# Feed-forward of a decoder layer: gatherings and sortings as two half DMAs on SyncE and GpSimd, with halves exchanged, and the next inputs' reads issued after the sums

## The chip, the cores and the metric

The kernel runs on one core of a Trainium2 chip. A core has a matrix engine (TensorE, PE in the profile, with its weight loads as PEld), a vector engine (VectorE, DVE), a scalar engine (ScalarE, ACT), a general engine (GpSimd, POOL) and an engine that only issues and waits (SyncE, SP). Each works through its own instructions in order; semaphores tie them together. Transfers (DMAs) are issued here by SyncE and GpSimd, and run on the 16 DMA engines of the core. SBUF, the core's memory, has 128 partitions; PE writes to PSUM, whence VectorE or ScalarE copies.

The metric is the device time of one execution in microseconds: the median of the runs is 610.52 us (three runs, 610.5 to 610.85).

## The reference, cut to what matters

The layer is self-attention, a decaying recurrence over a context, and a feed-forward, each with a residual and a layer norm. The change lies in the feed-forward, over 2048 tokens of 512 features:

```python
gate_w = spline_reconstruct(gate_cp, INTER, HIDDEN)   # cubic interpolation of few control points
up_w = spline_reconstruct(up_cp, INTER, HIDDEN)       # INTER = 2048, HIDDEN = 512
down_w = spline_reconstruct(down_cp, HIDDEN, INTER)
gate = jnp.einsum('bsh,ih->bsi', hidden_states, gate_w)
up = jnp.einsum('bsh,ih->bsi', hidden_states, up_w)
inter = jax.nn.silu(gate) * up
return jnp.einsum('bsi,hi->bsh', inter, down_w)
```

The weights are piecewise cubic polynomials along their rows. The kernel uses this: a row times a vector is a few exact products near the breaks of the polynomial plus moments of the vector over the pieces.

## The kernel before, in words

**Plan.** `ffn_plan` (line 55) is Python that runs before the kernel is built. It orders the 2048 intermediate features into 16 tiles of 128 and makes the tables: `up_taps` and `down_taps` (for the weights), `mom_f` (for the moments of the inputs) and `sum_f` (for the moments of the intermediates).

**Blocks.** The tokens are worked in four blocks b = 0..3 of 512 tokens (`GT`). All arrays are float32. The attention comes first; its last stage also makes the inputs of blocks 0 and 1.

**Inputs of a block.** `inputs(b)` (line 700) transposes the normed tokens on PE, writes them to memory off the core (`xd`; mostly issued by GpSimd, a few rows by SyncE), forms moments on PE and writes these too (`md`, by GpSimd). The input tile `xg` of a block, 128 partitions by 8 x 512 numbers, is read back from both: `windows` (line 683) issues four reads of `xd`, into 44 partitions of each half, and `moments` (line 694) two reads of `md`, into 20 partitions of each half. All six are on SyncE. For blocks 0 and 1 they are issued at once; for blocks 2 and 3 they are put into the list `reads`. `xg` has two buffers.

**Loop over the blocks** (lines 940 to 972; the order of the instructions of each engine is the order in which this Python calls them, since `Ordered` keeps the program order):

- For j = 0..7, `gate_up` (line 842) makes two tiles of `inter`: four matmuls for the gate and four for the up projection from `xg[:, j]`, silu on ScalarE, product on VectorE. `gather` (line 858) then issues, on SyncE, one DMA for each of the two tiles: it spreads the tile's 128 partitions over 16 partitions (r, r+8, ...) of `nat`, eight rows of 512 numbers to each. In blocks 1 and 2, one piece of `inputs(b+1)` follows each j; block b therefore makes the inputs of block b+1.
- Then the list `reads` is emptied: in blocks 1 and 2 this issues the six reads of the next block's `xg`.
- For t = 0..15, `exact` (line 865) adds four matmuls of tile t to the four outputs `y`. In blocks 1 to 3, at t = 0..3 the chain `outcome` (line 907) of the block before is started: transposes on PE, residual and norm on VectorE, ScalarE and GpSimd (`va`, `rs`), and a DMA `out<-o` on SyncE.
- At t = 7 come `residual(b)` (line 921), which later lets GpSimd copy the residual in 36 instructions (`x2p<-x`), and four calls of `into_sums` (line 875): eight matmuls `ps_s` each from `nat` and the table `sf`, a copy out of PSUM to `sum`, and a DMA `fin<-sum` on SyncE which sorts the 128 rows into 32 partitions of `fin` (called `sorted_` in the code).
- After t = 15, `finish` (line 894) adds eight matmuls `y<-fin` from the sorted sums and copies `y` out of PSUM.

The lines that the change edits are these:

```python
nc.sync.dma_start(out=nats[b, g][r::NSUM], in_=inters[b, t])   # gather
nc.sync.dma_start(out=sorted_[b][v::ND], in_=o)                # into_sums
while reads:                                                   # the loop, before t = 0
    reads.pop(0)()
```

Here `NSUM` is 8, `ND` is 4 and `K2` is 64. A DMA on SyncE takes one of eight completion semaphores in turn, so an issue waits until the DMA eight places before it has landed.

Of the kernel before, what the change touches and what calls it, by code (L numbers as in the profile page):

```python
# [17 lines left out]
P = 128  # L18
# [10 lines left out]
ND = 4  # L29
NTILE = INTER // P  # L30
NSUM = 8
# [5 lines left out]
K2 = 64  # L37
# [17 lines left out]
def ffn_plan():  # L55
# [9 lines left out]
    t = np.linspace(0.0, NCTRL - 1.0, n, dtype=np.float64)  # L65
# [10 lines left out]
    for d in range(ND):  # L76
# [4 lines left out]
        for j in range(-1, 18):  # L81
            b = np.clip(np.ceil(at + period * j - 1e-9).astype(int), 0, INTER)
# [56 lines left out]
    def covers(u, d):  # L139
        return range(BASE[u][d], BASE[u][d] + NSEG - (u == 0))  # L140
# [47 lines left out]
    def taps(sample, k):  # L188


        f = sample * step - k
        b = np.stack(
            [
                -0.5 * f + f**2 - 0.5 * f**3,
                1.0 - 2.5 * f**2 + 1.5 * f**3,
                0.5 * f + 2.0 * f**2 - 1.5 * f**3,
                -0.5 * f**2 + 0.5 * f**3,
            ]
        )
        return b, np.stack([np.clip(k + a, 0, NCTRL - 1) for a in (-1, 0, 1, 2)])  # L200
# [12 lines left out]
    for t in range(NTILE):  # L213
# [3 lines left out]
        for s in range(5):  # L217
            a, b = edges[2 * s], edges[2 * s + 1]
# [13 lines left out]
        b, i = taps(rows * D + places[:, None], piece[rows * D + within])  # L232
        b = b * (places < D)[None, :, None]
# [12 lines left out]
    for t in range(NTILE):  # L246
        rows = parts[t]
        for d in range(ND):
            q = slice(d * 32, (d + 1) * 32)
            sample = outs[d][None, :] * INTER + rows[q, None]  # L250
            dn_b[:, q, t * P : (t + 1) * P], dn_i[:, q, t * P : (t + 1) * P] = taps(sample, piece[sample])
        for p, i in enumerate(rows):
            u = p % NSUM
            r = t % NSUM + NSUM * (p // NSUM)
            for d in range(ND):
                if d == p // 32:
                    continue
                s = seg_of[d][i]
                if i in ALONE:
                    free = [s for s in range(NSEG) if s not in covers(0, d) or segs[d][s][0] == segs[d][s][1]]  # L260
                    taken = alone.setdefault(d, [])
                    taken.append(i)
                    x = free[(len(taken) - 1) // 4] * 4 + (len(taken) - 1) % 4
                    sums[r, t // NSUM * NSUM + u, x * ND + d] = 1.0
                else:
                    x = (s - BASE[u][d]) * 4 + np.arange(4)
                    sums[r, t // NSUM * NSUM + u, x * ND + d] = fact[d][s][1][i - segs[d][s][0]]
    for u in range(NSUM):
        for d in range(ND):
            col = slice((NTILE + d) * P, (NTILE + d + 1) * P)  # L270
            for s in range(NSEG):
                a, b = segs[d][BASE[u][d] + s]
                at, inner = fact[d][BASE[u][d] + s][0], np.full(4, min(a, INTER - 1))
                if u == 0 and (s not in covers(0, d) or a == b):
                    at, inner = np.zeros(4), np.zeros(4, np.int64)
                    for k in range(min(4, len(alone[d]))):
                        at[k] = inner[k] = alone[d].pop(0)
                r = ((u % 2 * 16 + s * 4 + np.arange(4)) * 4 + u // 2)[:, None]
                c = np.arange(col.start, col.stop)[None, :]
                inner = piece[outs[d][None, :] * INTER + inner[:, None]]  # L280
                dn_b[:, r, c], dn_i[:, r, c] = taps(outs[d][None, :] * INTER + at[:, None], inner)
# [34 lines left out]
def decoder_kernel(ctx: ExitStack, tc: tile.TileContext, x, xT, ctxT, wq, wkT, wvT, woT, wdownT, wup, decay, up_taps, down_taps, mom_f, sum_f, out, plan):  # L316
    nc = tc.nc
# [27 lines left out]
    nc = Ordered(tc)  # L345
    units, chains = [], []

    def slot():

        for c in list(chains):  # L350
            if next(c, c) is c:
                chains.remove(c)

    def fill(n):

        for i in range(n):
            if units:
                next(units[0][1])
                units[0][2] -= 1
                if not units[0][2]:  # L360
                    units.pop(0)
            if i % 2:
                slot()
                some_taps()
# [205 lines left out]
    def output(n, qc):  # L570

        ps = ps_mm.tile([P, D], F32, tag="mm", name="ps_o")
        for c in range(DC):
            nc.tensor.matmul(
                ps,
                lhsT=yTs[n][c // 2][:, c % 2, qc * P : (qc + 1) * P],
                rhs=w_o[:, c, :],
                start=(c == 0),
                stop=(c == DC - 1),
            )  # L580
            if c < DC - 1:
                yield
        h1 = rows.tile([P, D], F32, tag="row", name="h1")
        s1 = small.tile([P, 1], F32, tag="s1", name="s1")
        nc.vector.scalar_tensor_tensor(h1, ps, 1.0, xs[n][qc], ALU.mult, ALU.add, accum_out=s1)
        chains.append(norms(n, qc, h1, s1))
        yield
# [93 lines left out]
    xgs, reads = {}, []  # L681
# [70 lines left out]
    for s, (g, bb, quad) in enumerate(steps):  # L752
# [8 lines left out]
        if quad == 0 and n:  # L761
            load_rows(n - 1)
            o = [["o", output(n - 1, qc), DC] for qc in range(2)]
# [76 lines left out]
    inters, ys, sorted_, xps, nats = {}, {}, {}, {}, {}  # L840

    def gate_up(b, j):

        pgs, pus = [], []
        for w, pool, tag, to in ((wg, ps_mm, "mm", pgs), (wu, ps_big, "big", pus)):
            for h in range(2):
                at = slice(h * K2, (h + 1) * K2)
                ps = pool.tile([P, GT], F32, tag=tag, name="pg" if w is wg else "pu")
                nc.tensor.matmul(ps, lhsT=w[at, j * P : (j + 1) * P], rhs=xgs[b][at, j, :], start=True, stop=True)
                to.append(ps)  # L850
        for h in range(2):
            sg = work.tile([P, GT], F32, tag="sg", name="sg")
            nc.scalar.activation(sg, pgs[h], AF.Silu)
            inter = work.tile([P, GT], F32, tag="inter", name="inter", bufs=NTILE)
            nc.vector.tensor_tensor(inter, pus[h], sg, ALU.mult)
            inters[b, 2 * j + h] = inter

    def gather(b, t):

        g, r = t // NSUM, t % NSUM  # L860
        if not r:
            nats[b, g] = work.tile([P, NSUM, GT], F32, tag=f"nat{g}", name="nat", bufs=1)
        nc.sync.dma_start(out=nats[b, g][r::NSUM], in_=inters[b, t])

    def exact(b, t):

# [8 lines left out]
    def into_sums(b, v):  # L875

        if v == 0:
            sorted_[b] = late.tile([P, ND, GT], F32, tag="fin", name="fin")
        acc = ps_mm.tile([P, GT], F32, tag="mm", name="ps_s")
        for g in range(NTILE // NSUM):  # L880
            for a in range(2):
                u = 2 * v + a
                nc.tensor.matmul(
                    acc[a * K2 : (a + 1) * K2, :],
                    lhsT=sf[:, g * NSUM + u, :],
                    rhs=nats[b, g][:, u, :],
                    start=(g == 0),
                    stop=(g == NTILE // NSUM - 1),
                )
        o = work.tile([P, GT], F32, tag="inter", name="sum", bufs=NTILE)  # L890
        (nc.vector.tensor_copy if v % 2 else nc.scalar.copy)(o, acc)
        nc.sync.dma_start(out=sorted_[b][v::ND], in_=o)

    def finish(b):
        y = late.tile([P, ND, GT], F32, tag="ys", name="ys")
# [40 lines left out]
    def settle():  # L936
        while chains:
            slot()

    for b in range(NG):  # L940
        if 0 < b < NG - 1:
            units.append(["i", inputs(b + 1), 2 * DC])
        for j in range(NTILE // 2):
            gate_up(b, j)
            gather(b, 2 * j)
            gather(b, 2 * j + 1)
            if b:
                slot()
                fill(1)
        if b == 0:  # L950
            fill(2 * DC)
        while reads:
            reads.pop(0)()
        for t in range(NTILE):
            exact(b, t)
            if b and t < TC:
                chains.append(outcome(b - 1, t))
            slot()
            if b == 0 and t < 5:
                slot()  # L960
            if b == 0 and t == 4:
                settle()
                done.close()
                late = ffn["mom"] = ctx.enter_context(tc.tile_pool(name="late", bufs=1, side="right"))
            if t == 7:
                settle()
                chains.append(residual(b))
                for v in range(NSUM // 2):
                    into_sums(b, v)
        assert not units  # L970
        finish(b)
    for t in range(TC):
# [55 lines left out]
```

## Time and profile before

The profiled execution took 612.27 us, with a span of 610.5 us from the first to the last instruction and a mean granted TensorE clock of 0.993.

| engine | busy us | share of the span | instructions |
|---|---|---|---|
| PE | 584.3 | 96% | 3346 |
| PEld | 288.8 | 47% | 3346 |
| DVE | 334.5 | 55% | 742 |
| ACT | 276.9 | 45% | 820 |
| POOL | 210.1 | 34% | 479 |

The feed-forward begins at 401.3 us. Its stages, by PE, start at these times (us):

| block | `gate_up` | `exact` t=0 | sums `ps_s` | `exact` t=8 | `finish` |
|---|---|---|---|---|---|
| 0 | 401.27 | 423.15 | 431.83 | 438.85 | 445.93 |
| 1 | 449.56 | 471.28 | 482.03 | 489.05 | 497.75 |
| 2 | 501.35 | 523.07 | 533.83 | 540.85 | 550.06 |
| 3 | 555.36 | 569.30 | 581.05 | 588.07 | 595.15 |

DMAs of the feed-forward, from the table of issues:

| DMA | issued by | count | KB each |
|---|---|---|---|
| `nat<-inter` (gatherings) | SyncE | 64 | 256 |
| `fin<-sum` (sortings) | SyncE | 16 | 256 |
| `xg<-xd` (windows, four blocks) | SyncE | 8 and 8 | 616 and 88 |
| `xg<-md` (moments, four blocks) | SyncE | 8 | 320 |
| `out<-o` | SyncE | 16 | 256 |
| `xd<-x2T` | GpSimd | 16 | 250 to 256 |
| `md<-mom` | GpSimd | 4 and 4 | 512 and 128 |

How to read the rows of the profile: a group of instructions is told as engine, line, operation, output tile, inputs, shape, number, and in brackets the idle time of the engine before it with what ended that. All instructions stand under line 308, a helper that records them, so tiles tell them apart. A table of stretches gives the busy time of each engine, the granted TensorE clock, the mean busy share of the 16 DMA engines and the GB/s that they moved. The chain of waits goes back from the last instruction to what released it, step by step.

### The profile page before, as it was taken

How to read it: one execution, taken by the hardware profiler on the slowest of the kernel's cores; microseconds unless marked ns; L12 is line 12 of the kernel's file. 1: busy time of each engine (PE TensorE's matmuls, PEld its weight loads, DVE VectorE, ACT ScalarE, POOL GpSimd, SP SyncE). 2: the span in 40 equal slices, each digit the busy share in tenths (PEclk: the TensorE clock that was granted, in tenths of full speed). 3: DMA queues.
4: the chain of work that ended last, by engine and by line, in shares of the span. 5: the costliest groups of instructions: out<-in, count | busy, mean ns of one | idle time of the engine just before them, and what ended most of it. 6: DMA issues, size and time to landing. Idle time of an engine off the chain costs nothing.

```text
span 610.5 us, 9688 instructions
## 1 busy us (share of the span) xinstructions
PE 584.3 (96%) x3346; PEld 288.8 (47%) x3346; DVE 334.5 (55%) x742; ACT 276.9 (45%) x820; POOL 210.1 (34%) x479
## 2 busy tenths in 40 slices
PE   8999999998999999999999898899999989999993
PEld 3544555555455555555556455444343333334432
DVE  0204545657875666786665778867635316504614
ACT  0115634647555456565556666664233214304402
POOL 0001986264636334644420301202511611350152
PEclk9999999999999999999999999999999999998998
DMA  8104253044124114314101653588129849973931
GB/s 301 52 0 155 89 182 92 20 139 138 53 68 141 35 53 160 118 52 139 47 23 53 176 141 108 156 195 177 71 71 246 226 121 236 222 208 79 217 119 69
DMA packets 39984, 75.50 MB, mean 124 GB/s; under 512 B 3936, under 2 KB 8288, under 8 KB 39936
## 3 DMA queue, kind: packets, MB, share of 16 engines
q1 hardware_dynamic: 36880, 66.94, 40.1%
q0 software_dynamic: 2048, 6.77, 3.4%
q10 hardware_dynamic: 1008, 1.18, 0.6%
q8 instruction: 26, 0.43, 0.3%
q14 instruction: 22, 0.18, 0.1%
HBM read 42.86 MB, written 11.04 MB: 88 GB/s over the span
## 4 chain that ended last, share of the span: by engine, by line
PE 72%; DVE 10%; issue 7%; DMA 5%; ACT 3%; POOL 2%; SPq 0%; POOLq 0%; DVEq 0%; ACTq 0%
PE ps_k L308 9%; PE ps_v L308 9%; PE ps_o L308 8%; PE y L308 8%; PE ps_q L308 7%; PE tr_e L308 6%; PE sc L308 5%; PE av L308 5%; PE pg L308 4%; PE pu L308 3%; DVE nmax L308 3%; PE ps_s L308 2%; DMA xg<-md 2%; ACT e L308 2%; PE ps_mom L308 2%
## 5 line engine op out<-in xcount | busy, mean ns | idle before, releaser
L308 ACT ACTIVATE e<-sc,nmax 128x256 f32<-128x256 f32 x256 | 120.3, 481 | 101.4 <-DVE nmax L308 101.3
L308 DVE TENSOR_REDUCE nmax<-sc 128x2 f32<-128x512 f32 x128 | 84.4, 681 | 73.6 <-PE sc L308 67.6
L308 POOL TENSOR_TENSOR taps<-taps 128x256 f32<-128x256 f32 (+1 forms) x144 | 89.0, 618 | 32.1 <-DMA taps<-in_down_taps 24.2
L308 PE MATMUL tr_e<-ident,e 128*128 128x128 f32 x512 | 68.3, 276 | 0.6 <-DVE eT L308 0.4
L308 PEld LDWEIGHTS tr_e<-ident,e 128*128 128x128 f32 x512 | 56.9, 140 | 25.2 <-issue 22.5
L308 PE MATMUL y<-inter,wd 32*128 32x512 f32 x512 | 63.6, 605 | 0.0
L308 PE MATMUL ps_o<-w_o,yT 128*128 128x512 f32 x128 | 60.0, 600 | 1.9 <-DVE eT L308 1.6
L308 PE MATMUL ps_k<-xT_g,w_k 128*128 128x512 f32 x128 | 58.7, 600 | 0.6 <-DVE eT L308 0.6
L308 PE MATMUL ps_v<-w_v,xT_g 128*128 128x512 f32 x128 | 58.6, 598 | 0.4 <-DVE eT L308 0.4
L308 PE MATMUL ps_q<-xT_g,w_q 128*128 128x512 f32 x128 | 58.2, 596 | 0.0
L308 POOL TENSOR_SCALAR va<-ss 128x1 f32<-128x1 f32 x32 | 7.0, 220 | 144.5 <-ACT x L308 85.8
L308 DVE TENSOR_TENSOR inter<-pu,sg 128x512 f32<-128x512 f32 x64 | 41.2, 686 | 26.6 <-PE pu L308 13.7
L308 ACT ACTIVATION_READ_ACCUMULATOR e<-sc,nmax 128x1 f32 x256 | 53.3, 208 | 0.0
L308 POOL TENSOR_TENSOR rs<-va,neghalf 128x1 f32<-128x1 f32 x48 | 28.0, 584 | 70.3 <-DVE va L308 67.6
L308 ACT ACTIVATE sg<-pg 128x512 f32<-128x512 f32 x64 | 36.1, 596 | 30.1 <-PE pg L308 29.9
L308 DVE COPY eT<-tr_e 128x512 f32<-128x512 f32 x64 | 43.7, 682 | 0.5 <-PE tr_e L308 0.4
L308 PE MATMUL av<-eT,v_g 128*32 128x256 f32 x512 | 36.7, 385 | 5.0 <-ACT eT L308 2.7
L308 PEld LDWEIGHTS y<-inter,wd 32*128 32x128 f32 x512 | 25.2, 184 | 28.9 <-issue 24.4
L308 ACT COPY eT<-tr_e 128x512 f32<-128x512 f32 x64 | 37.5, 586 | 2.4 <-PE tr_e L308 2.4
L308 PE MATMUL sc<-k_g,q_g 32*128 32x256 f32 x512 | 37.4, 401 | 0.2 <-ACT e L308 0.2
L308 POOL TENSOR_TENSOR r<-r 128x1024 f32<-128x1024 f32 x8 | 15.2, 1896 | 63.3 <-DMA r<-in_ctxT 63.3
L308 PEld LDWEIGHTS ps_v<-w_v,xT_g 128*128 128x128 f32 x128 | 23.1, 190 | 25.5 <-issue 24.3
(97 smaller groups left out, 734.0 us busy)
## 6 DMA issues: line engine op xcount, KB each, us to landing
nat<-inter SPq DMA_DIRECT2D x64, 256.0 KB
taps<-in_down_taps SPq DMA_DIRECT2D x40, 256.0 KB
taps<-in_up_taps SPq DMA_DIRECT2D x16, 384.0 KB
xg<-xd SPq DMA_DIRECT2D x8, 616.0 KB
r<-in_ctxT SPq DMA_DIRECT2D x8, 512.0 KB
x_t<-in_x SPq DMA_DIRECT2D x16, 256.0 KB
fin<-sum SPq DMA_DIRECT2D x16, 256.0 KB
out<-o SPq DMA_DIRECT2D x16, 256.0 KB
```

Source lines behind the costliest of these rows:

```text
L308: return lambda *a, **k: self.tc.keep_in_program_order(f(*a, **k))
```

## The change

Three things are edited.

- In `gather`, the one DMA becomes two. SyncE takes the tile's partitions 0 to 63 and spreads them over partitions 64+r, 72+r, ... of `nat`; GpSimd takes partitions 64 to 127 and spreads them over r, 8+r, ... below 64. So the halves change places. The table `sum_f`, whose rows stand for the partitions of `nat`, is turned by 64 rows to match.
- In `into_sums`, the sorting DMA becomes two in the same manner, and the `down_taps` rows that meet the sorted sums change halves too.
- The loop over `reads` moves from before t = 0 to the end of t = 7, behind the four calls of `into_sums`.

```diff
@@ ffn_plan
-            r = t % NSUM + NSUM * (p // NSUM)
+            r = (t % NSUM + NSUM * (p // NSUM) + P // 2) % P
...
-                r = ((u % 2 * 16 + s * 4 + np.arange(4)) * 4 + u // 2)[:, None]
+                r = (((u + 1) % 2 * 16 + s * 4 + np.arange(4)) * 4 + u // 2)[:, None]
@@ gather
-        nc.sync.dma_start(out=nats[b, g][r::NSUM], in_=inters[b, t])
+        nc.sync.dma_start(out=nats[b, g][K2 + r :: NSUM], in_=inters[b, t][:K2])
+        nc.gpsimd.dma_start(out=nats[b, g][r:K2:NSUM], in_=inters[b, t][K2:])
@@ into_sums
-        nc.sync.dma_start(out=sorted_[b][v::ND], in_=o)
+        nc.sync.dma_start(out=sorted_[b][K2 + v :: ND], in_=o[:K2])
+        nc.gpsimd.dma_start(out=sorted_[b][v:K2:ND], in_=o[K2:])
@@ the loop over the blocks
-        while reads:
-            reads.pop(0)()
         for t in range(NTILE):
             exact(b, t)
...
                 for v in range(NSUM // 2):
                     into_sums(b, v)
+                while reads:
+                    reads.pop(0)()
```

## The prediction

> **What bounds the kernel now.** I read the busy table first: TensorE (PE) is busy for 96% of the span, the next engine for 55%. So the time is PE's program order plus the few gaps in it, and a change pays only where PE stands still. Next, PE's timeline in the feed-forward, where the change lies. Columns: start, duration, instruction group, in brackets the idle time before it and what ended it.
>
> ```profile
> 482.03 7.09 PE L308 MATMUL ps_s<-nat,sf 128*64 128x512 f32 x32
> 489.05 7.15 PE L308 MATMUL y<-inter,wd 32*128 32x512 f32 x64
> 497.75 3.67 PE L308 MATMUL y<-fin,wd 128*128 128x512 f32 x8 [1.55 <-DMA fin<-sum]
> ...
> 533.83 7.09 PE L308 MATMUL ps_s<-nat,sf 128*64 128x512 f32 x32
> 540.85 7.15 PE L308 MATMUL y<-inter,wd 32*128 32x512 f32 x64
> 550.06 5.37 PE L308 MATMUL y<-fin,wd 128*128 128x512 f32 x8 [2.07 <-DMA fin<-sum]
> 555.36 1.13 PE L308 MATMUL pg<-xg,wg 64*128 64x512 f32 x4
> ```
>
> These are blocks b=1 and b=2: sums (`ps_s`), exact matmuls of t=8..15, `finish` (`y<-fin`), and the next block's `gate_up` (`pg`), which reads `xg`. Only here does PE wait for something the change touches: 1.55 and 2.07 us for the sorted sums. After the longer gap the eight `finish` matmuls took 5.37 instead of 3.67 us. Blocks 0 and 3 have no such gap: from the start of `ps_s` to the end of `finish` they need 449.56-431.83 = 17.7 and 598.69-581.05 = 17.6 us. What delays the sums is in the chain of waits (start, duration, what) and in SyncE's queue:
>
> ```profile
> 531.48 13.62 DMA xg<-md
> 545.10 0.02 issue
> 545.12 0.02 SPq L308
> 545.13 0.03 issue
> 545.16 4.76 DMA fin<-sum
> 549.93 0.14 issue
> 550.06 5.37 PE y L308 x8
> ```
>
> ```profile
> SPq L308 <- DMA xg<-md: 4.5, 2, 2.5
> SPq L308 <- DMA xg<-xd: 3.1, 2, 2.3
> ```
>
> The second fence is the queue's waits between 524 and 548 us (total, times, longest). The sums' DMAs are issued behind the six reads of the next inputs, and SyncE waits for those reads to land before it issues the later sums. So the next block's data arrive first, with time to spare, and this block's sums last.
>
> **The change, part by part.**
>
> *Reads behind the sums: what goes.* The sums no longer queue behind reads. Block 0 shows the undisturbed queue: four sum issues from 435.45 to 440.21, the last ending 8.4 us after `ps_s` began (431.83), and `finish` followed without a wait. Then blocks 1 and 2 reach their next `gate_up` 17.7 us after the start of `ps_s`: at 499.7 instead of 501.35, and at 551.5 instead of 555.36. Gain, if nothing is late next: 1.6+3.8 = 5.4 us, which is the two gaps and 1.70 us of slow matmuls.
>
> *Reads behind the sums: what is late next.* `gate_up` of block b+1 with j=0 needs both halves of `xg`, rows from the windows and from the moments, so the last of the six reads. SyncE works in order; each sum issue waits for its copy out of PSUM, which waits for PE. So the first read goes out 8.4 us after `ps_s` begins: at 490.4 (block 1) and 542.2 (block 2), where now it goes at 473.02 and 525.22. PE will want the data at 499.7 and 551.5: the cover is 9.3 us. How long do the reads take? By the table of DMA issues they move 2x88+2x616+2x320 = 2,048 KB. Nearest rows, stretches with almost only such reads in flight (the windows at 387.5, the moments at 395 with two row loads and at 541):
>
> ```profile
> 387.50:390.00 2.50, 2.50 (x10) 1.25 (x10) 2.40 (x10) 1.68 (x7) 0.56 (x1) 1.00 0.76 151
> 395.00:401.00 6.00, 5.71 (x37) 2.98 (x35) 3.15 (x10) 2.49 (x6) 1.39 (x3) 1.00 0.69 151
> 541.00:543.00 2.00, 2.00 (x20) 0.98 (x24) 0.66 (x1) 0.00 (x0) 0.83 (x4) 1.00 0.85 150
> 561.00:577.00 16.00, 16.00 (x86) 6.74 (x83) 10.42 (x22) 7.84 (x16) 1.48 (x4) 1.00 1.07 211
> ```
>
> The last number is GB/s. At 151 GB/s, 2.097 MB take 13.9 us, plus 1.2 us from issue to first data (block 3's first gathering is issued at 558.15, the DMA engines move nothing until 559.3): 15.1 us. The other end is the present itself: 525.22 to 531.48+13.62 = 545.10, 19.9 us, with the tail of the gatherings and the writes of `md` in its way, which will be done by then. I take 17. The last read then lands at 507.4 and 559.2, and PE stands 7.7 us each time. Against the present starts of `gate_up`: 507.4-501.35 = +6.0, 559.2-555.36 = +3.9. Together +9.9 us, the 5.4 us of gain already inside.
>
> *The clock after the new gaps.* The 1.55 us gap left the granted clock at 1.00; after the 2.07 us gap it was 0.69 over 549.9 to 555.36, and 1.70 us were lost. The Trainium skill ("TensorE: Matmul & The Clock Gate", section "Why this matters for your kernels") asks for no idle gaps over about 3 us. By that rule the 2.07 us gap would not explain the slow matmuls, their 1.70 us would stay, and my sum would be 1.7 higher; the row says that the gap made them slow, so I let them go with it. The new gaps of 7.7 us are past both limits: I charge each the measured 1.70 us, +3.4. Ends: nothing, and twice that each.
>
> *Gatherings in halves.* All 64 `nat<-inter` DMAs become 64 half-size ones on SyncE and 64 on GpSimd. SyncE keeps its number of issues, about 0.55 us each. GpSimd gains 64 issues; its nearest row, `md<-mom` and `xd<-x2T`, has 0.64 and 0.56 us. In a block's `gate_up` that is 16 x 0.56 = 9 us beside at least 13.9 us in which GpSimd does at most 2.3 us of work. Queued behind a half that waits for its `inter` are the `xd` writes and, in the exact loop, the norm's `va`/`rs`, which come later anyway; the late reads give `xd` time. Without this cover the norm chain is delayed, whose `h3`/`o` nobody on PE waits for until the end of the kernel. What limits a gathering is the fourth row: 211 GB/s, 16 engines more than full, so 262,144 bytes in 1.24 us a tile, while `gate_up` makes a tile in 0.87 us. A rule of the skill speaks against halves: "DMA: Bandwidth & Descriptors" ("Why a DMA increments its semaphore by 16 and not by 1") says that a DMA runs on the largest number of engines up to 16 that divides the slowest dimension of both sides. Whole gatherings write 16 partitions, halves 8: eight engines instead of sixteen. At the row's 13.2 GB/s per engine, SyncE's 131,072 bytes take 1.24 us on eight. If GpSimd's half runs on the other eight, or shared engines go faster because two queues feed them, a tile still takes 1.24 us; if both sit on the same eight at that pace, 2.5 us. I take 1.24: the row's share over full says that engines wait on each other's writes, not that each is at its own limit. In block 3 the cover is thin (16 x 1.24 after 559.3 is 579.1, sums begin at 581.05), in the others 5 us or more. Cost 0; ends -0 (no `ps_s` waits for `nat` now) and +2.
>
> *Sortings in halves.* SyncE's and GpSimd's last halves go out 8.4 us after `ps_s` begins; GpSimd's DMAs land 4.3 us after issue (`xd<-x2T`), `finish` begins 14.1 us after: 1.4 us to spare. Behind them on GpSimd are the 36 copies of `residual`, 8.4 us, today at 580.90 in block 3; they would end at 589.5+8.4 = 598 where `h` needs them at 600.07. Cost 0; if that 2 us of cover goes, as much at the end.
>
> *Tables `sum_f` and `down_taps`.* Rows change places, same sizes: 0, one answer.
>
> Sum: +9.9+3.4 = +13.3 us. The profiled execution took 612.27 us with a span of 610.5; it becomes 625.6. The median shown is 610.52, so my forecast is **623.8 us**.
>
> **Rivals.**
>
> 1. *The reads land in time (faster).* For it: the sums really are delayed by reads, and PE's gaps are named after them. If the reads ran at the 292 GB/s that the mix of 491 to 494 us reached, they would need 7.2+1.2 us, under the cover of 9.3; all 5.4 us would be gained: 605 us. It decides at a read time of about 11 us: at 10.9 the new gaps are 1.6 us and the balance is (490.4+10.9-501.35)+(542.2+10.9-555.36) = -2.3; from some 11.4 on the gaps pass 2.07 us, the clock goes too, and it is slower. Against: 15.1 us is the low end, and at 151 GB/s the windows' 1,408 KB alone take 9.5+1.2 us.
>
> 2. *Halved gatherings become the bound.* At 2.5 us a tile they end 40 us after their first data: about 14 us after the present start of `ps_s` in block 0, 12 in each of 1 and 2, 18 in block 3; some 55 us, with the late reads 55+13 more, 679 us. For it: the engine count of the skill. Against: the over-full engines above, and a second queue.
>
> 3. *No change that can be told.* The order is changed but the reads overlap the last sums enough that new gaps come to what the old ones were (a read time near 11): 610.5 us.
>
> **Numbers.** Forecast 0.86, rival 1 0.06, rival 2 0.05, rival 3 0.03. Range: read time 15.1 to 19.9 us (-3.8, +5.8), clock (-3.4, +3.4), gatherings (+2), not all at one end: 616 to 633, with about 0.15 outside. About 0.2% is what this kernel's measurement can tell from no change. Faster 0.07, same 0.03, slower 0.90.
>
> **What would show it.** Right: no wait of `y<-fin` for `fin<-sum` in blocks 1 and 2, a wait of about 8 us of `pg` (or its weight load) for `xg<-md` at the start of blocks 2 and 3, none at block 1; a granted clock under 1.00 just after; `xg<-xd` issued after `fin<-sum`. Halves right: `ps_s` without waits. Wrong: `pg` starts without a wait (rival 1), or `ps_s` waits for `nat` (rival 2), or the waits at `pg` are under 5 us.

## The result and the profile after

The changed kernel takes 644.81 us (median of four runs, 643.4 to 645.05) against 610.6 us for the kernel before: a ratio of 1.0555, 95% interval 1.0537 to 1.0573. It is slower by 34 us. The forecast had the sign, but its 623.8 us and its range up to 633 us were too low. The profiled execution took 645.03 us with a span of 643.1 us, 32.6 us more than the span before.

First the timeline of PE after the change, the lines that answer to those shown of before (start, duration, group, idle time before it and what ended that):

```profile
432.94 1.08 PE L308 MATMUL ps_s<-nat,sf 128*64 128x512 f32 x4
434.54 6.23 PE L308 MATMUL ps_s<-nat,sf 128*64 128x512 f32 x28 [0.52 <-DMA nat<-inter]
...
485.96 6.23 PE L308 MATMUL ps_s<-nat,sf 128*64 128x512 f32 x28 [1.00 <-DMA out<-o]
492.12 7.15 PE L308 MATMUL y<-inter,wd 32*128 32x512 f32 x64
499.20 3.70 PE L308 MATMUL y<-fin,wd 128*128 128x512 f32 x8
509.07 3.24 PE L308 MATMUL pg<-xg,wg 64*128 64x512 f32 x3 [6.17 <-issue]
...
547.56 7.20 PE L308 MATMUL ps_s<-nat,sf 128*64 128x512 f32 x32
...
561.77 3.70 PE L308 MATMUL y<-fin,wd 128*128 128x512 f32 x8
571.51 2.04 PE L308 MATMUL pg<-xg,wg 64*128 64x512 f32 x2 [6.04 <-DMA xg<-md]
573.75 1.19 PE L308 MATMUL pg<-xg,wg 64*128 64x512 f32 x1 [0.20 <-DMA xg<-md]
...
606.52 8.71 PE L308 MATMUL ps_s<-nat,sf 128*64 128x512 f32 x28 [4.81 <-DMA nat<-inter]
```

The waits of `finish` for the sums are gone: both `y<-fin` groups now follow without a gap and take 3.70 us. In their place `gate_up` (`pg`) of blocks 2 and 3 waits some 6 us for the inputs, and then 1.5 to 1.7 us more in its first matmuls, whose second half of `xg` lands with the last read. New are the waits of `ps_s`, worst in block 3; the forecast had `ps_s` without waits, and named such waits as a sign that it was wrong. In block 1 the row names `out<-o` as what ended the wait. `ps_s` reads only `nat` and `sf`, and the DMAs of SyncE share their completion semaphores in turn, so what it waited for is a gathering there too. In block 3 the chain of waits runs through the gatherings:

```profile
584.88 9.98 DMA nat<-inter
...
594.93 11.35 DMA nat<-inter
606.28 0.24 issue
606.52 8.71 PE ps_s L308 x28
```

The last gathering is issued on SyncE only at 594.93, when an earlier one has landed, and lands at 606.28; GpSimd's last half had landed at 601.09. In the table of stretches, here cut where the clock changes, the granted clock is the third figure from the right:

```profile
505.74:519.40 13.66, 10.33 (x20) 3.59 (x20) 1.38 (x2) 2.87 (x5) 1.77 (x3) 0.50 0.39 80
519.40:521.00 1.60, 1.60 (x10) 0.92 (x10) 1.34 (x3) 0.00 (x0) 0.34 (x1) 1.00 0.25 86
570.59:577.42 6.83, 5.72 (x12) 2.26 (x14) 0.69 (x1) 1.19 (x2) 0.50 (x1) 0.50 0.18 37
577.42:579.00 1.58, 1.58 (x10) 0.76 (x8) 1.18 (x2) 1.18 (x2) 0.51 (x2) 1.00 0.38 56
```

The clock falls to half during each gap and stays there after PE has started again at 509.07 and 571.51: for 10.3 us in block 2 and 5.9 us in block 3. PE does not work through all of that time, since it waits once more for the second half of `xg`; from there, 511.12 and 573.75, it is 8.3 and 3.7 us. And one cost lies behind all work. The kernel ends with a `DRAIN` on each engine's sequencer; the rows of GpSimd's before the change (line 1023) and after it (line 1025), and of SyncE's after it, give min/median/max in ns, then the first and last start in us:

```profile
L1023 POOLq DRAIN  x3: 40/93/2644, 606.0 to 610.2; - x3
```

```profile
L1025 POOLq DRAIN  x3: 40/93/9182, 633.1 to 642.8; - x3
L1025 SPq DRAIN  x3: 7/7/7, 636.8 to 642.6; - x3
```

GpSimd's longest starts when the last norm is issued. It took 2.644 us before, and ended about 1 us before the last output had landed. It takes 9.182 us now and ends at 642.3, while SyncE, which waits for the outputs, gets to its first `DRAIN` at 636.8. So the whole kernel waits for GpSimd's.

The 32.6 us, by comparing when PE reaches the same place in both traces (rounded rows):

| where | us |
|---|---|
| start of the kernel (the attention begins later and keeps that distance) | +1.1 |
| `ps_s` waits for `nat`: blocks 0, 1, 2, 3 | +0.7, +1.2, +0.1, +7.5 |
| waits of `finish` gone, with the slow matmuls behind the second | -1.6, -3.8 |
| `gate_up` of blocks 2 and 3 waits until both halves of `xg` are there | +7.8, +7.8 |
| half clock in these `gate_up` | +4.5, +2.3 |
| `exact` of block 3 | -0.6 |
| end of the kernel, behind PE | +5.5 |

Of the 7.5 us in block 3, 4.8 us are the wait and 2.5 us the half clock behind it (28 matmuls in 8.71 instead of 6.23 us).

### The profile page after: what moved, and what is told of

Same layout as the page of the kernel before. It is cut to its first block, busy times and chain, and to the rows that moved or that the text cites. A ratio compares the mean times of both kernels' runs of the same rounds, so it can differ in the third digit from the quotient of the medians.

```text
span 643.1 us, 9961 instructions
## 1 busy us (share of the span) xinstructions
PE 596.1 (93%) x3346; PEld 293.5 (46%) x3346; DVE 335.6 (52%) x742; ACT 277.2 (43%) x820; POOL 254.2 (40%) x559
## 5 line engine op out<-in xcount | busy, mean ns | idle before, releaser
L308 POOL DMA_DIRECT2D nat<-inter x64 | 36.3, 568 | 70.5 <-DVE inter L308 58.0
L308 PE MATMUL pg<-xg,wg 64*128 64x512 f32 x128 | 47.2, 672 | 12.4 <-DMA xg<-md 6.2
L308 PE MATMUL pu<-xg,wu 64*128 64x512 f32 x128 | 43.9, 635 | 0.0
```

What stands on the lines that cost most here:

```text
L308: return lambda *a, **k: self.tc.keep_in_program_order(f(*a, **k))
```

## The experiments

**Late reads alone.** From the kernel before:

```diff
-        while reads:
-            reads.pop(0)()
         for t in range(NTILE):
...
                     into_sums(b, v)
+                while reads:
+                    reads.pop(0)()
```

> Only the reads move behind the sums; gatherings and sortings are whole, on SyncE. Theory (three separate costs: late reads with a long slow clock, slow half gatherings, a longer end on GpSimd): the span goes from 610.5 to about 627 us: waits of finish for the sums gone (-5.3), two waits of gate_up for the reads (+12), some 10 us of half clock after them; ps_s waits for nothing, the end after the last output as before (3.3 us). Rival (the late reads cause nearly all, by pushing the gatherings too): 635 us or more, with ps_s waiting for nat. Rival (the clock costs 1.7 us for each gap, as I had it): about 621 us.

Measured: 628.36 us, ratio 1.0284 (1.0255 to 1.0312), span 627.8 us. PE's timeline in it:

```profile
496.13 3.70 PE L308 MATMUL y<-fin,wd 128*128 128x512 f32 x8
505.82 2.04 PE L308 MATMUL pg<-xg,wg 64*128 64x512 f32 x2 [6.00 <-issue]
508.15 1.19 PE L308 MATMUL pg<-xg,wg 64*128 64x512 f32 x1 [0.28 <-DMA xg<-md]
...
598.35 7.09 PE L308 MATMUL ps_s<-nat,sf 128*64 128x512 f32 x32
```

`finish` does not wait, `gate_up` waits, `ps_s` takes its 7.09 us without a wait, and the `DRAIN` is 2.644 us as before. So the late reads are worth 17 us, half of the loss, and they do not cause the slow gatherings. While PE worked, the clock was at half from 505.8 to 517.6 and again from 568.6 to 575.7.

**Halves alone.** The gather and sort edits of the change with their tables; the reads stay before t = 0.

> Only the halves; the reads stay before t = 0. Theory: ps_s waits for nat (5 us and a slow clock in block 3, about 1 us in blocks 0 and 1), the end is 5.5 us longer, no wait of gate_up for xg: 625 to 629 us. Rival (the halves only suffer where the late reads shift them): 616 us, the longer end alone.

Measured: 637.77 us, ratio 1.0453 (1.0421 to 1.0485), span 635.1 us, more than the theory said.

```profile
504.30 5.33 PE L308 MATMUL y<-fin,wd 128*128 128x512 f32 x8 [5.53 <-DMA fin<-sum]
...
542.04 1.08 PE L308 MATMUL ps_s<-nat,sf 128*64 128x512 f32 x4
544.32 6.23 PE L308 MATMUL ps_s<-nat,sf 128*64 128x512 f32 x28 [1.19 <-DMA nat<-inter]
562.82 5.08 PE L308 MATMUL y<-fin,wd 128*128 128x512 f32 x8 [5.20 <-DMA fin<-sum]
...
599.38 7.93 PE L308 MATMUL ps_s<-nat,sf 128*64 128x512 f32 x28 [4.78 <-DMA out<-o]
```

No `pg` waits. But with reads in the old place the slow gatherings delay the reads behind them, and these the sums: in block 1 the last read goes out at 486.97 instead of 483.01 and the last sum at 499.28 instead of 492.40. `finish` waits over 5 us twice. The two parts therefore do not add: 24.6 us of halves and 17.3 us of reads make 32.6 us together, since the late reads spare the halves these waits. The wait in block 3 and the `DRAIN` of 9.182 us are those of the full change.

**Late reads, with PE kept busy.** The first experiment, and after `finish`:

```diff
+        if 0 < b < NG - 1:
+            ps = ps_mm.tile([P, GT], F32, tag="mm", name="ps_fill")
+            for _ in range(16):      # 8 in the second of the two
+                nc.tensor.matmul(ps, lhsT=ident, rhs=sorted_[b][:, 0, :], start=True, stop=True)
```

> The first experiment with 16 idle matmuls of 512 columns behind finish in blocks 1 and 2, whose result nobody reads. Theory (the gap makes the clock slow, and the slow clock lasts since PE is not busy enough to leave it): the granted clock is 1.00 through gate_up, the reads land at the same place, about 10 us less than the first experiment: 617 us. Rival (gate_up is slow for another cause, such as the DMAs): no gain, 627 us.

> Late reads alone with 8 idle matmuls behind finish in blocks 1 and 2 (16 took 13.9 us each time instead of the 6.9 us I had meant, and PE was late by itself). Theory (half clock after a gap costs about 4 to 5 us in each block when nothing fills it): gate_up starts when the reads land, about 8 us after finish, at full clock; 619 to 621 us against 627.8 for the late reads alone. Rival (the clock is not the cause): 627 us or more.

Measured: 634.97 us with 16 and 625.05 us with 8 idle matmuls (one run each; spans 633.2 and 622.2 us, 627.8 us without). My first size was wrong: one float32 matmul of this form is two instructions and takes 0.86 us, so sixteen fill 13.9 us where the gap is 7.8 us. PE then was late by the filler itself, and the total says nothing on the clock. The stretches of both `gate_up` do; with 16, then with 8:

```profile
514.10:535.90 21.80, 21.80 (x100) 8.07 (x99) 11.73 (x19) 9.85 (x18) 2.26 (x4) 1.00 0.83 209
578.05:592.00 13.95, 13.95 (x67) 6.14 (x66) 9.03 (x14) 8.94 (x16) 0.00 (x0) 1.00 0.75 154
```

```profile
507.70:529.50 21.80, 21.44 (x93) 8.09 (x92) 10.90 (x17) 9.28 (x17) 2.26 (x4) 1.00 0.76 197
566.20:581.00 14.80, 14.50 (x64) 7.21 (x64) 9.76 (x15) 9.16 (x16) 0.00 (x0) 1.00 0.74 153
```

The clock is 1.00 and `gate_up` takes the 21.8 and 14 us it took before the change, with the same DMAs beside it; the last row also has the wait for the second half of `xg` in it. That the gap makes `gate_up` slow is shown. With 8 fillers the span is 5.6 us shorter than with the bare gap, though PE does 14 us of idle work. That is less than the 7 to 9 us expected, but the feed-forward of this run also began 1.1 us later. From the arrival of the second half of `xg` to the start of `exact`, blocks 2 and 3 are 4.5 and 2.4 us shorter, the size that the half clock has in the full change.

**Sortings in halves alone.** Only the sort edit with its table.

> Only the sortings in exchanged halves; gatherings whole on SyncE, reads before t = 0. Theory (the end on GpSimd grows with the number of its DMAs, 24 before and 104 after, 6.5 us for 80 of them): with 40 it is 1.3 us longer; the waits of finish for fin stay, since SyncE's halves are still behind the reads: 611.8 us. Rival (any use of GpSimd's queue late in the kernel makes the long end): 616 us.

Measured: 614.55 us, one run; span 612.8 us, 2.3 us more. The drain is 1.3 us longer, as expected; with 40 GpSimd DMAs it reads

```profile
L1024 POOLq DRAIN  x3: 40/102/3953, 608.0 to 612.5; - x3
```

Behind PE the kernel ends only 0.3 us later, since before the change the drain ended some 1 us before the last output had landed. The waits of `finish` grew by 0.6 and 0.9 us, and the feed-forward began 0.4 us later. Against the forecast's 0 for this part that is small, and from one run.

**Gatherings cut otherwise.** Four variants, with the reads before t = 0. Halves that stay in their places, gatherings and sortings (tables as before):

```diff
+        nc.sync.dma_start(out=nats[b, g][r:K2:NSUM], in_=inters[b, t][:K2])
+        nc.gpsimd.dma_start(out=nats[b, g][K2 + r :: NSUM], in_=inters[b, t][K2:])
```

> Halves on SyncE and GpSimd, but each half stays in its own half of the partitions (tables as before); reads before t = 0. To be compared with the halves that change places (635.1 us span). Theory (each half writes eight partitions and so runs on fewer DMA engines; the places do not matter): the same waits of ps_s for nat, 632 to 638 us. Rival (the exchange makes halves cross each other's ports): ps_s hardly waits, 616 to 622 us. Rival (the exchange helps): slower than 640 us.

Halves by columns, sortings whole:

```diff
+        nc.sync.dma_start(out=nats[b, g][r::NSUM, :, : GT // 2], in_=inters[b, t][:, : GT // 2])
+        nc.gpsimd.dma_start(out=nats[b, g][r::NSUM, :, GT // 2 :], in_=inters[b, t][:, GT // 2 :])
```

> Gatherings split by columns: SyncE takes the first 256 columns of all 128 partitions, GpSimd the others; sortings whole, reads before t = 0. Theory (too few engines per half): with 16 partitions written by each DMA the pace is that of whole gatherings, ps_s waits for nothing, and only the end is longer by 64 x 0.082 = 5.2 us: 616 us. Rival (two queues on the same engines slow each other): ps_s waits for nat as in the halves by partitions, 628 us or more.

The change's two gathering halves both on SyncE (`nc.sync` in both lines), and whole gatherings all on GpSimd (`nc.gpsimd` in the old line), sortings whole in both:

> Gatherings in exchanged halves, both issued by SyncE; sortings whole, reads before t = 0. Theory (a half of eight partitions runs on eight engines, and SyncE's always on the same eight): the sixteen tiles of block 3 take about 40 us instead of 20, ps_s waits 10 us or more in every block: over 650 us. The end as before (3.3 us). Rival (the slow part is GpSimd's queue or its sharing): ps_s hardly waits, about 612 to 616 us.

> Whole gatherings, all issued by GpSimd; the rest as before the change. Theory (engine count and number of GpSimd DMAs are what costs): the pace of whole gatherings stays, 1.2 us a tile, ps_s waits under 1 us, and the end is 5.2 us longer; the sums no longer stand behind gatherings in SyncE's queue: 614 to 616 us. Rival (GpSimd's queue is slow by itself): ps_s waits 5 us or more in block 3, 625 us or more.

| variant | time (one run) | span | wait of `ps_s` in block 3 | GpSimd DMAs | longest `DRAIN` |
|---|---|---|---|---|---|
| before | 610.6 (median) | 610.5 | 0 | 24 | 2.644 |
| exchanged halves | 637.77 (median) | 635.1 | 4.78 | 104 | 9.182 |
| halves in their places | 639.75 | 637.8 | 5.59 | 104 | 9.182 |
| halves by columns | 613.63 | 611.9 | 0 | 88 | 7.877 |
| exchanged halves, both on SyncE | 648.27 | 646.5 | 9.39 | 24 | 2.642 |
| whole, on GpSimd | 620.11 | 618.3 | 0 | 88 | 7.875 |

From PE's timelines, block 3, of the halves by columns and of the halves on SyncE alone:

```profile
578.23 7.09 PE L308 MATMUL ps_s<-nat,sf 128*64 128x512 f32 x32
```

```profile
616.25 7.88 PE L308 MATMUL ps_s<-nat,sf 128*64 128x512 f32 x28 [9.39 <-DMA out<-o]
```

This decides three things. Two queues are not the trouble: columns on two queues have no wait of `ps_s`. GpSimd's queue is not the trouble: whole gatherings on it have none either, and halves without GpSimd are the worst of all. The exchange is not the trouble, and no cure that can be told: the one run of straight halves lies within the runs of exchanged ones (637.11 to 640.52). What the three slow variants share is a DMA that reads 64 and writes 8 partitions.

The stretches say what that shape does. Halves on SyncE alone, in block 3, while they queue up (the last figures are the busy share of the DMA engines and GB/s):

```profile
586.00:600.00 14.00, 14.00 (x71) 5.75 (x68) 9.04 (x18) 6.71 (x13) 0.69 (x2) 1.00 0.54 127
```

The whole gatherings of the kernel before, in the same block (561 to 577), had 1.07 and 211 GB/s. So with halves only about half of the 16 DMA engines are busy, though more are queued. The trace agrees in two more ways. Of SyncE's packets mostly 8 or 9 are in flight at a time, where whole gatherings have 16 or more. And the landing of a whole gathering steps its semaphore 16 times, that of a SyncE half 8 times. For this variant the expectation was over 650 us, from 40 us for the gatherings of a block. It came out a little lower: they took 33.1 us, or 2.1 us a tile. Eight engines are faster each than sixteen (127/8 = 15.9 against 13.2 GB/s), but not twice as fast.

Whole gatherings on GpSimd missed their expectation of 614 to 616 us: besides the longer drain, `finish` waits 2.60 us in blocks 1 and 2, each time with a slow spell after it.

**The change with columns.** The changed kernel with the gatherings by columns as above, its sortings, reads and number of GpSimd DMAs kept.

> The changed kernel with the gatherings cut by columns instead of partitions (each DMA reads 128 and writes 16 partitions); sortings in exchanged halves and late reads as in the change, and as many GpSimd DMAs. Theory (the halves of eight partitions are slow for their number of engines): ps_s waits for nothing, the waits for the reads, the half clock after them and the long end stay: 643.1 less some 9.6 us, 633 to 634 us. Rival (with late reads the gatherings are late however they are cut): 640 us or more.

Measured: 633.27 us, one run, span 631.3 us.

```profile
596.36 7.09 PE L308 MATMUL ps_s<-nat,sf 128*64 128x512 f32 x32
610.45 3.70 PE L308 MATMUL y<-fin,wd 128*128 128x512 f32 x8
```

`ps_s` waits nowhere, the waits of `pg` (5.78 and 6.46 us) and the drain (9.180 us) stay. The shape of the half gatherings costs the change 11.8 us of span, somewhat more than the 9.6 us that its waits add up to. Two other differences between the two traces are of the size of the rest: here the feed-forward begins 1.2 us earlier, and the spell of half clock in block 2 is shorter (10.2 instead of 13.7 us).

**Whole sortings on ScalarE's queue.** What the changed order was good for, the early sums, without late reads and without GpSimd:

```diff
-        nc.sync.dma_start(out=sorted_[b][v::ND], in_=o)
+        nc.scalar.dma_start(out=sorted_[b][v::ND], in_=o)
```

> The kernel before, with the four whole sortings of a block issued by ScalarE instead of SyncE; gatherings whole on SyncE, reads before t = 0. Theory (the sums were late because they stood behind the reads in SyncE's queue, and only GpSimd's DMAs lengthen the end): finish no longer waits in blocks 1 and 2 (-1.6 and -3.7), the reads land early enough, the end stays 3.3 us: 605 to 606 us. Rival (the sums share the DMA engines with the reads whoever issues them, so they land no earlier): 609 to 611 us.

Measured: 607.58 us against 611.0 us, ratio 0.9941 (0.9923 to 0.9959); span 605.6 us. It is 0.6% faster than the kernel before, a small gain but clear of noise.

```profile
496.57 3.70 PE L308 MATMUL y<-fin,wd 128*128 128x512 f32 x8
500.20 1.13 PE L308 MATMUL pg<-xg,wg 64*128 64x512 f32 x4
```

Neither `finish` nor `gate_up` waits, and the drain is 2.644 us. The sums were late for their place behind the reads in SyncE's queue, not for a lack of DMA capacity.

## Why the prediction was right or wrong

- **Stall for the late reads: right.** Forecast: first read issued 8.4 us after the start of `ps_s`, 17 us of reading, PE standing 7.7 us twice, the old waits gone. Measured in block 2: first read 9.2 us after the start of `ps_s`, last one landed 16.9 us later. PE stood 7.8 us twice; with the old waits taken off it is +10.2 us where the sum had +9.9. Late reads alone showed the same place. PE starts on the first half of `xg` some 2 us before the last read lands, which the forecast had not seen; nothing is gained by it, since the matmuls behind stop for the second half.
- **Clock after the gaps: right mechanism, wrong size.** The term was 1.70 us each, taken from the one slow spell in the trace before. It measured 4.5 and 2.3 us in the two `gate_up`, and the fillers show that the gap is the cause. The 1.70 us came from one spell of 3.41 us at half clock (551.00 to 554.41). The spells here are whole multiples of that: 13.65 us in block 2, 10.3 of them behind PE's restart, and 6.83 us in block 3. So one spell was a poor measure of the next: block 2 went past the upper end of twice 1.70, and the two together (6.8 us) just reach it. The 2.07 us gap was no limit either. A gap of 2.15 us in the run with sortings in halves and one of 3.25 us with halves on SyncE left the clock at 1.00. The Trainium skill ("TensorE: Matmul & The Clock Gate", section "What's actually happening") has PE back at full clock after some 3.4 us of sustained work. Counted from where both halves of `xg` are there, block 3 agrees (3.7 us); block 2 does not (8.3 us), and the measurement decides. Why it took longer in block 2, where transposes stand between the matmuls, was not tried and stays open.
- **Gatherings in halves: wrong.** This is the step that failed most. The forecast weighed the Trainium skill's rule ("DMA: Bandwidth & Descriptors", section "Why a DMA increments its semaphore by 16 and not by 1") that a DMA runs on the largest number of engines up to 16 that divides the slowest dimension of both sides, found 1.24 to 2.5 us a tile, and took 1.24 because the share over full seemed to say that engines wait on each other; so its cost was 0. Measured are 9.6 us, a pace between the two. In block 3 the first gathering goes out at 576.65 and the last lands at 606.28: 29.6 us for what took 22.6 us (558.15 to 580.73 by the same reading). That is 1.85 us a tile instead of 1.41, the time from issue to landing included. Block 3 paid most of the 9.6 us. Its cover was thinner than the forecast's sum said: the last whole gathering landed at 580.73, not 579.1, 0.3 us before `ps_s` began. The upper end of +2 did not follow from its own 2.5 us a tile, which stood in the text as a rival with 0.05. The rule on the number of engines holds here: the run with halves on SyncE alone keeps about half of them busy. The row's share over full had told something real, since eight engines are faster each than sixteen, but not enough to make up for half of them. With both queues, SyncE's halves land last in every block, 4 to 5 us after GpSimd's in three of the four; how the halves of the two queues share engines was not taken apart.
- **End of the kernel: a term put at nothing, without a reason.** The forecast priced GpSimd's 80 new DMAs at 0.56 us of issue each and hid these. It did not ask what else grows with their number. The drain at the end does: 2.644, 3.953, 7.877 and 9.182 us for 24, 40, 88 and 104 DMAs, which is 0.082 us for each more, in a straight line. With 24 it ended 1 us before the last output had landed; the other 80 lengthened it by 6.5 us and so cost 5.5 us of span.
- **Sortings in halves: right in the change** (no wait of `finish`, `h` not delayed), but for their share of the longer drain; alone the span was 2.3 us longer.
- **Start: +1.1 us, unexplained.** In the experiments too the first `ps_s` begins from 0.2 us earlier to 1.1 us later than in the kernel before, whatever was edited, so I don't count it to the change.
- Together: 13.3 us forecast, +0.3 for the stall, +3.4 for the clock, +9.6 for the gatherings, +5.5 for the end, +1.1 for the start, -0.6 in `exact`: 32.6 us.
- **Rivals.** The one with 0.05, gatherings as the bound, was true in kind at about a sixth of its size (9.6 us where it had some 55), and came on top of the likeliest case instead of in its place. My cases excluded each other where the costs could add.

## What to carry to other kernels

Moving a transfer behind another in one queue only exchanges which is late: compare its whole duration with the time until its first use, and give the urgent one a queue of its own instead, where one is free. Before cutting a DMA in two, look at what each piece reads and writes: two pieces of 64 and 8 partitions were slower than one of 128 and 16, two pieces by columns were not. The mean busy share of the DMA engines tells it: 0.54 while DMAs were queued meant that about half of the engines did nothing. And count what a queue pays at the end of the kernel for each DMA, not only when it is issued.

## What the runs showed of the hardware that was not expected

- GpSimd's drain at the end of the kernel grew by 0.082 us for every DMA that GpSimd had issued in the whole kernel (24 to 104 of them, four counts on a line), though the last of them had landed before `finish` of block 3 read its data, some 11 us earlier in the changed kernel (622.24 against 633.1 us). The size of the DMAs did not matter: 64 whole gatherings and 64 halves by columns gave 7.875 and 7.877 us.
- Spells of half clock came in steps of 3.41 us: 3.41 us in the kernel before, 6.83 and 13.65 in the changed one, 10.24 in the late reads alone (565.42 to 575.66). The length of the gap before did not alone decide: gaps of 2.15 and 3.25 us cost nothing, one of 2.07 us cost 1.70 us.
- A DMA that reads 64 and writes 8 partitions kept about half of the 16 DMA engines busy (share 0.54, 127 GB/s) where one of 128 and 16 partitions kept them all (1.07, 211 GB/s).
- A float32 gathering by columns, 1 KB a row, on two queues was as quick as the whole one with 2 KB rows (22.8 and 22.6 us for the tiles of block 3); it even let `finish` wait less (0.73 and 1.17 us instead of 1.55 and 2.07), and only the drain made that kernel slower.
